# Gathered edge rows on Trainium2: a second wait in each batch of four fetches

## The chip, the cores and the metric

The kernel runs on one core of a Trainium2 chip. Its engines are PE (TensorE, matrix products, with PEld for the loading of weights), DVE (VectorE), ACT (ScalarE), POOL (GpSimd, which here issues the indirect fetches) and SP (SyncE, which issues plain transfers). Every engine works through its own list of instructions in order, and waits on semaphores for the others. The metric is the device time of one launch in microseconds (us), less being better. Times given for "runs" are medians of several launches; a profile is one launch taken by the hardware profiler.

## The reference

The reference is one layer of a graph network with 12,500 nodes of 160 channels and 400,000 edges, sorted by destination. Cut to what matters:

```python
h = relu(layernorm(x))                               # [12500, 160]
y0 = h[:, :64] @ W_l1_0 * a / 8                      # per node, a = node attribute
y1 = einsum('nuc,uv->nvc', h1, W_l1_1) * a / sqrt(32)
w  = silu(edge16 @ fc_W1 / 4) @ fc_W2 / 8            # per edge, 192 weights
mid_a = w_a * y0[src] * e0                           # four products per edge
mid_d = w_d * sum_c(y1[src] * e1) / sqrt(3)
mid_b = (w_b * y0[src])[:, :, None] * e1[:, None, :]
mid_c = (w_c * e0)[:, :, None] * y1[src]
z = segment sum of (mid_a, mid_d, mid_b, mid_c) over dst
out = x + C_S * (self part of h) + C_X * (z @ W_l2) * a
```

The part that takes the time is the middle: for each edge the row of `y` that belongs to its source node is fetched, multiplied by the edge's own weights, and added up over the edges that end in the same node.

## The kernel before

First the kernel writes the mapped node rows `y_d` to HBM (some 115 us). Then comes the main loop, which is what the change touches.

The edges are cut into 3125 tiles of 128, and four tiles (`GT = 4`) make a batch; there are 782 batches, numbered `b`. For each batch the following is done, by functions that are written out in program order in one loop over `b` and keep that order on every engine (the scheduling is manual).

- `gather(b)` on POOL: four indirect fetches (L570), one per tile; each brings the 128 rows of 160 floats that belong to a tile's sources from `y_d` into one slot of the buffer `yg`. There are six such buffers. Sixteen of the 782 batches (`xs_of`) are not fetched but worked out from `x`.
- `hidden_pair(s)` on PE (L583) and ACT (L588): the first layer of the edge network, for four batches at a time. It stands behind the sums of every fourth batch.
- `weigh(b)` on PE (L603): the second layer, two products into the PSUM tile `pw`; ACT adds five columns of edge data to it (L525).
- `products(b)` on DVE: the one-hot matrix `sel` (L617, L619) and the product rows `pr` out of `pw` and `yg` (L530, then L534 twice). This is the only reader of the fetched rows.
- `sums(b)` on PE (L633): four products `sel` times `pr`, one per tile, added up in the PSUM tile `pz`. A window of 3 to 24 tiles shares one `pz`. Behind the last tile of a window DVE turns the sums out of PSUM (L639, L640 into `za`).
- `linear`, `add` and `accumulate` once for every four windows (L646, L650, L658, L669): the last linear layer and the addition into `acc`.

In one pass for `b` the order of the code is: `weigh(b + 2)`, `linear` or `add` if due, `products(b + 1)`, `sums(b)`, `gather(b + 4)` and, for every fourth `b`, `hidden_pair`. So rows are fetched four batches ahead (`AHEAD = 4`), products are made one ahead of the sums, and weights two ahead.

What sets the pace of the fetches is one wait. The first of the four fetches of batch `b` waits on a semaphore of PE until the last product of the sums of batch `b - 4` has ended; the other three follow it on POOL's queue without a wait on PE:

```python
if k == 0 and b - AHEAD in summed:
    tc.add_manual_dep(fetch.ins, summed[b - AHEAD], ...)
```

`summed[b]` holds the name of the last product that `sums(b)` issued.

## Time and profile before

| what | value |
|---|---|
| median of three runs | 4708.81 us (4700.06 to 4720.77) |
| the profiled execution, its own time | 4710.64 us |
| its span, first to last instruction | 4708.8 us |
| fetches of the main loop on POOL (L570) | 3061, 2901.9 us busy |
| sums on PE (L633) | 1950.3 us busy |
| weights on PE (L603) | 1233.8 us busy |
| mean granted clock of TensorE | 0.906 |

How to read it: a busy time is the sum of an engine's instruction times. An "idle before" time is how long the engine stood still ahead of a group of instructions, with the event that ended the idleness behind the arrow; "issue" means that nothing in the profile released it, and "remote" or "another core or an unknown queue" that the releaser was not found among the recorded instructions near the release. The start of a matmul is recorded and its end is modelled. The granted clock of TensorE is 1 at full rate; in this trace it is either 1 or one half.

### The profile page before, as it was taken

How to read it: one execution, taken by the hardware profiler on the slowest of the kernel's cores; microseconds unless marked ns; L12 is line 12 of the kernel's file. 1: busy time of each engine (PE TensorE's matmuls, PEld its weight loads, DVE VectorE, ACT ScalarE, POOL GpSimd, SP SyncE). 2: the span in 40 equal slices, each digit the busy share in tenths (PEclk: the TensorE clock that was granted, in tenths of full speed). 3: DMA queues.
4: the chain of work that ended last, by engine and by line, in shares of the span. 5: the costliest groups of instructions: out<-in, count | busy, mean ns of one | idle time of the engine just before them, and what ended most of it. 6: DMA issues, size and time to landing. Idle time of an engine off the chain costs nothing.

```text
span 4708.8 us, 46910 instructions
## 1 busy us (share of the span) xinstructions
PE 3891.7 (83%) x14078; PEld 2542.2 (54%) x14078; DVE 2736.7 (58%) x6877; ACT 581.6 (12%) x1845; POOL 2968.3 (63%) x3145
## 2 busy tenths in 40 slices
PE   7788888888788787887888888888888888888888
PEld 6455555555555455555555555555555555555555
DVE  5555555555555555555555656556556666666665
ACT  5111111111111101101110101111011111111100
POOL 5666666666666666666666666666666666666665
PEclk8889999999999998988888989998989998998889
DMA  7222222222222222222222222222222222222224
GB/s 192 69 63 65 66 66 65 66 67 64 60 64 67 66 69 67 67 66 67 70 68 62 65 63 67 66 68 63 63 66 65 68 64 63 65 64 67 59 62 117
DMA packets 262471, 328.58 MB, mean 70 GB/s; under 512 B 82888, under 2 KB 212216, under 8 KB 262216
## 3 DMA queue, kind: packets, MB, share of 16 engines
q0 software_dynamic: 150128, 256.23, 20.5%
q1 hardware_dynamic: 111590, 69.02, 5.2%
q8 instruction: 116, 1.90, 0.2%
q14 instruction: 139, 1.14, 0.1%
q10 hardware_dynamic: 498, 0.30, 0.0%
HBM read 307.67 MB, written 17.61 MB: 69 GB/s over the span
## 4 chain that ended last, share of the span: by engine, by line
PE 66%; another core or an unknown queue 15%; issue 7%; DVE 7%; ACT 2%; ACTq 1%; POOL 0%; DMA 0%; DVEq 0%; SPq 0%; POOLq 0%
PE pz L633 31%; PE pw L603 19%; PE px L646 6%; PE px L583 3%; DVE pr L534 2%; PE px L658 2%; DVE pr L530 1%; ACT hT L588 1%; ACTq L525 1%; DVE za L640 1%; DVE za L639 1%; PE po L457 1%; PE px L704 1%; POOL yg L570 0%
## 5 line engine op out<-in xcount | busy, mean ns | idle before, releaser
L570 POOL DMA_INDIRECT yg<-y_d,src_q x3061 | 2901.9, 948 | 1681.5 <-issue 795.2
L633 PE MATMUL pz<-pr,sel 128*128 128x320 f32 x6250 | 1950.3, 457 | 17.6 <-DVE za L640 15.2
L633 PEld LDWEIGHTS pz<-pr,sel 128*128 128x128 f32 x6250 | 1243.5, 204 | 542.6 <-issue 94.9
L603 PE MATMUL pw<-w,hT 128*128 128x384 f32 x3126 | 1233.8, 519 | 208.7 <-DVE pr L534 135.6
L603 PEld LDWEIGHTS pw<-w,hT 128*128 128x128 f32 x3126 | 590.3, 198 | 734.3 <-issue 375.5
L639 DVE STREAM_TRANSPOSE za<-pz 128x160 f32<-128x160 f32 x598 | 206.5, 345 | 1298.9 <-PE pz L633 551.3
L534 DVE TENSOR_TENSOR pr<-pw,yg 128x384 f32<-128x384 f32 x1532 | 773.5, 546 | 0.0
L530 DVE TENSOR_TENSOR pr<-pw,yg 128x512 f32<-128x512 f32 x766 | 523.2, 683 | 126.8 <-DMA yg<-y_d,src_q 118.3
L646 PE MATMUL px<-wo,za 128*128 128x160 f32 x1500 | 320.2, 376 | 294.4 <-ACT hT L588 198.2
L619 DVE TENSOR_TENSOR sel<-own,pw 128x512 f32<-128x512 f32 x782 | 536.9, 687 | 28.1 <-issue 1.2
L646 PEld LDWEIGHTS px<-wo,za 128*128 128x128 f32 x1500 | 290.2, 246 | 364.7 <-ACT hT L588 226.5
L525 ACT ACTIVATE pw<-ev 128x20 f32<-128x20 f32 x782 | 149.6, 191 | 2624.1 <-PE pw L603 970.4
L588 ACT ACTIVATE hT<-px 128x512 f32<-128x512 f32 x391 | 218.5, 595 | 968.9 <-remote 648.9
L583 PE MATMUL px<-xe,w 32*128 32x512 f32 x782 | 268.9, 658 | 66.2 <-ACT os L648 38.8
L617 DVE TENSOR_TENSOR own<-iota,pw 128x128 f32<-128x128 f32 x782 | 200.0, 256 | 177.1 <-ACT pw L525 133.8
L640 DVE STREAM_TRANSPOSE za<-pz 32x160 f32<-32x160 f32 x598 | 202.1, 338 | 20.5
L658 PE MATMUL px<-os,place 128*128 128x160 f32 x600 | 122.6, 332 | 79.0 <-ACT os L648 75.8
L669 DVE SCALAR_TENSOR_TENSOR acc<-px,a_sb,acc 128x160 f32 x300 | 113.9, 380 | 113.2 <-PE px L658 70.8
L658 PEld LDWEIGHTS px<-os,place 128*128 128x128 f32 x600 | 107.0, 211 | 131.8 <-ACT os L648 91.2
L583 PEld LDWEIGHTS px<-xe,w 32*128 32x128 f32 x782 | 70.9, 187 | 176.8 <-issue 95.7
L648 ACT ACTIVATE os<-px 128x160 f32<-128x160 f32 x150 | 45.3, 302 | 359.8 <-remote 168.4
L712 DVE SCALAR_TENSOR_TENSOR acc<-px,look,acc 128x160 f32<-128x160 f32 x98 | 32.9, 377 | 95.1 <-PE pz L633 39.7
(129 smaller groups left out, 1423.7 us busy)
## 6 DMA issues: line engine op xcount, KB each, us to landing
yg<-y_d,src_q POOLq DMA_INDIRECT x3061
xe<-in_e SPq DMA_DIRECT2D x784, 32.0 KB
xs<-in_x SPq DMA_DIRECT2D x48, 160.0 KB
acc<-in_x SPq DMA_DIRECT2D x11, 640.0 KB
y_d<-ys SPq DMA_DIRECT2D x11, 640.0 KB
out<-acc SPq DMA_DIRECT2D x11, 640.0 KB
raw<-in_e SPq DMA_DIRECT2D x32, 192.0 KB
src_q<-in_src SPq DMA_DIRECT2D x32, 48.0 KB
```

The source lines that it names most:

```text
L530: nc.vector.tensor_mul(pr[:, :n, :].rearrange("p t (x u) -> p t x u", x=2)[:, :, :, 0:M0], wt[:, :n, 0:NW].rearrange("p t (x u) -> p t x u ...
L534: nc.vector.tensor_mul(pr[:, :n, D * x + M0:D * (x + 1)].rearrange("p t (c u) -> p t c u", c=3), wt[:, :n, 96 * x + M0:96 * (x + 1)].unsqu ...
L570: fetch = nc.gpsimd.indirect_dma_start(out=yg[:, slot(t), :], out_offset=None, in_=y_d, in_offset=bass.IndirectOffsetOnAxis(ap=ev4[t // BL ...
L583: nc.tensor.matmul(ph, w1[r, :], xe[r, :], start=True, stop=True)
L588: nc.scalar.activation(hT, ph, AF.Silu, scale=1.0 / math.sqrt(FC_IN))
L603: nc.tensor.matmul(pw[:, 2 * k:2 * k + m, 0:NW], hT[:, o:o + P], w2[:, :m, :], start=True, stop=True)
L619: nc.vector.tensor_tensor(sel, own[:, :n, :].unsqueeze(2).to_broadcast([P, n, 4, WN]), wt[:, :n, NW:NW + 4].unsqueeze(3).to_broadcast([P, ...
L633: mm = nc.tensor.matmul(pz[:, 0:PC], sel[:, slot(t), :, :], pr[:, slot(t), :], start=o == 0, stop=last)
L639: nc.vector.transpose(zT[g][:, :, at_w], pz[:, D:PC].rearrange("p (k u) -> p k u", k=ZK))
L640: nc.vector.transpose(zT[g][0:32, :, at_w], pz[0:32, 0:D].rearrange("p (k u) -> p k u", k=ZK))
L646: nc.tensor.matmul(po[:m, :], za[:, k, :m], wo[:, k, :], start=k == 0, stop=k == ZK - 1)
L658: nc.tensor.matmul(ps[:, h, :], place[:m, h, :], os[:m, :], start=True, stop=True)
```

## The change

Two things change, both in the issue of the fetches.

First, the fetches are issued by half batches. Behind `sums(b)` stood the four fetches of batch `b + 4`. Now stand there the third and fourth fetch of batch `b + 3`, and then the first and second fetch of batch `b + 4`.

Second, the third fetch of a batch now waits too. The first fetch of batch `m` waits, as before, for the last product of `sums(m - 4)`; the third fetch of batch `m` waits for the second of the four products of `sums(m - 3)`, which the new table `halves` names.

```diff
+        halves = {}
...
-        def gather(b):
-            yg = ygp.tile([P, GT, D], F32, name="yg")
-            rows[b] = yg
-            for k, t in enumerate(tiles_of(b)):
+        def gather(b, part=slice(0, GT)):
+            if part.start == 0:
+                rows[b] = ygp.tile([P, GT, D], F32, name="yg")
+            yg = rows[b]
+            for k, t in list(enumerate(tiles_of(b)))[part]:
                 fetch = nc.gpsimd.indirect_dma_start(
...
-                if k == 0 and b - AHEAD in summed:
-                    tc.add_manual_dep(fetch.ins, summed[b - AHEAD],
+                of = {0: summed.get(b - AHEAD), 2: halves.get(b - AHEAD + 1)}.get(k)
+                if of is not None:
+                    tc.add_manual_dep(fetch.ins, of,
...
-                summed[b] = mm.ins.name
+                (halves if k == 1 else summed)[b] = mm.ins.name
...
             sums(b)
-            if b + AHEAD < NB and b + AHEAD not in xs_of:
-                gather(b + AHEAD)
+            for m, part in ((b + AHEAD - 1, slice(2, GT)), (b + AHEAD, slice(0, 2))):
+                if AHEAD <= m < NB and m not in xs_of:
+                    gather(m, part)
```

On POOL the place shown is the middle of the first fifth of the loop. `yg_4810` and `yg_4848` are the row buffers of two batches that follow each other; a DMASW name is the completion of an earlier fetch, DVE the readers of the buffer's former content, PE the sums. Before:

```order
L570 DMA yg_4810<-y_d_60,src_q_3744 128x160 [waits DMASW4_49,DVE_49,PE_49]
L570 DMA yg_4810<-y_d_60,src_q_3744 128x160 [waits DMASW5_49]
L570 DMA yg_4810<-y_d_60,src_q_3744 128x160 [waits DMASW6_49]
L570 DMA yg_4810<-y_d_60,src_q_3744 128x160 [waits DMASW7_49]
L570 DMA yg_4848<-y_d_60,src_q_3744 128x160 [waits DMASW0_49,DVE_49,PE_49]
L570 DMA yg_4848<-y_d_60,src_q_3744 128x160 [waits DMASW1_49]
L570 DMA yg_4848<-y_d_60,src_q_3744 128x160 [waits DMASW2_49]
L570 DMA yg_4848<-y_d_60,src_q_3744 128x160 [waits DMASW3_49]
```

The order of the fetches is the same now, and the third of each batch has a wait on PE of its own. After:

```order
L572 DMA yg_4810<-y_d_60,src_q_3742 128x160 [waits DMASW4_49,DVE_49,PE_49]
L572 DMA yg_4810<-y_d_60,src_q_3742 128x160 [waits DMASW5_49]
L572 DMA yg_4810<-y_d_60,src_q_3742 128x160 [waits DMASW6_49,PE_49]
L572 DMA yg_4810<-y_d_60,src_q_3742 128x160 [waits DMASW7_49]
L572 DMA yg_4848<-y_d_60,src_q_3742 128x160 [waits DMASW0_49,DVE_49,PE_49]
L572 DMA yg_4848<-y_d_60,src_q_3742 128x160 [waits DMASW1_49]
L572 DMA yg_4848<-y_d_60,src_q_3742 128x160 [waits DMASW2_49,PE_49]
L572 DMA yg_4848<-y_d_60,src_q_3742 128x160 [waits DMASW3_49]
```

761 of the 3061 fetches of the loop get this second wait, and no fetch moved in POOL's queue.

On PE the place shown is a fourth batch, with the weights (`pw`), the four sums (`pz`) and the pair of the first layer (`px` out of `xe`) behind them. Before:

```order
L603 MATMUL pw<-w_94,hT 128x2x192 [waits DVE_49,Activation_49]
L603 MATMUL pw<-w_94,hT 128x2x192
L633 MATMUL pz<-pr,sel 128x320 [waits PE_49]
L633 MATMUL pz<-pr,sel 128x320 x3
L583 MATMUL px<-xe,w_93 128x512 [waits DMAHW3_49,DMAHW2_49]
L583 MATMUL px<-xe,w_93 128x512 [waits DMAHW5_49,DMAHW4_49,Activation_49]
L603 MATMUL pw<-w_94,hT 128x2x192 [waits DVE_49]
```

The same rows stand there now, at line numbers that are three higher. After:

```order
L606 MATMUL pw<-w_94,hT 128x2x192 [waits DVE_49,Activation_49]
L606 MATMUL pw<-w_94,hT 128x2x192
L636 MATMUL pz<-pr,sel 128x320 [waits PE_49]
L636 MATMUL pz<-pr,sel 128x320 x3
L586 MATMUL px<-xe,w_93 128x512 [waits DMAHW3_49,DMAHW2_49]
L586 MATMUL px<-xe,w_93 128x512 [waits DMAHW5_49,DMAHW4_49,Activation_49]
L606 MATMUL pw<-w_94,hT 128x2x192 [waits DVE_49]
```

Nothing moved or was added on PE, DVE, ACT and SP, and their waits are the same; the second of the four sums now has a waiter on POOL.

## The prediction

> **What bounds the kernel now.** I read the page's sums by engine first, then the chain of waits, then the waits of POOL and DVE, and last a stretch of 40 us in order of time. The first fence has the engines' busy times and the chain that ended last, by engine, from the page.
>
> ```profile
> PE 3891.7 (83%) x14078; PEld 2542.2 (54%) x14078; DVE 2736.7 (58%) x6877; ACT 581.6 (12%) x1845; POOL 2968.3 (63%) x3145
> ...
> PE 66%; another core or an unknown queue 15%; issue 7%; DVE 7%; ACT 2%; ACTq 1%; POOL 0%; DMA 0%; DVEq 0%; SPq 0%; POOLq 0%
> ```
>
> No engine is full, and 15% of the chain, some 706 us of 4708.8, has no instruction at all to show for itself. POOL looks free. The next fence shows that it is not: the fetches as one group with their first and last start, the waits of POOL (total, times, longest), and the one wait for rows on DVE.
>
> ```profile
> L570 POOL DMA_INDIRECT yg<-y_d,src_q x3061: 940/947/1236, 115.6 to 4686.4; - x192
> L570 POOLq EVENT_SEMAPHORE  x798: 17/43/205, 102.2 to 4681.2; - x200
> ...
> POOL yg L570 <- issue: 795.2, 2541, 4.6
> POOL yg L570 <- PE pz L633: 372.5, 149, 7.2
> POOL yg L570 <- remote: 314.1, 131, 3.7
> POOL yg L570 <- PE pw L603: 85.0, 66, 4.9
> ...
> DVE pr L530 <- DMA yg<-y_d,src_q: 118.3, 70, 3.0
> ```
>
> Now POOL in order of time (start, length, idle before); left out are fetches like their neighbours.
>
> ```profile
> 2524.74 0.95 POOL L570 DMA_INDIRECT yg<-y_d,src_q  x1 [4.28 <-PE pz L633]
> 2525.99 0.95 POOL L570 DMA_INDIRECT yg<-y_d,src_q  x1 [0.30 <-issue]
> ...
> 2538.53 0.94 POOL L570 DMA_INDIRECT yg<-y_d,src_q  x1 [0.30 <-issue]
> 2541.93 0.95 POOL L570 DMA_INDIRECT yg<-y_d,src_q  x1 [2.46 <-remote]
> ...
> 2545.69 0.95 POOL L570 DMA_INDIRECT yg<-y_d,src_q  x1 [0.30 <-issue]
> 2549.32 0.95 POOL L570 DMA_INDIRECT yg<-y_d,src_q  x1 [2.68 <-PE pz L633]
> ...
> 2563.10 0.94 POOL L570 DMA_INDIRECT yg<-y_d,src_q  x1 [0.30 <-issue]
> 2566.58 0.94 POOL L570 DMA_INDIRECT yg<-y_d,src_q  x1 [2.54 <-remote]
> ```
>
> A fetch holds POOL for 0.95 us and the next starts 0.30 us later: one step is 1.25 us, a batch of four 5.0 us. 3061 steps are 3826 us, and from the first fetch to the last pass 4571 us. So POOL is taken for 84% of the main loop, and its real idleness is about 745 us, which the three waits on PE hold (372.5 + 314.1 + 85.0 in 346 waits, each with 0.30 us of its step). Twelve fetches in a row, three batches, is what stands between two waits in 2524.74 to 2538.53 and in 2549.32 to 2563.10.
>
> The same time on PE:
>
> ```profile
> 2531.80 1.53 PE L603 MATMUL pw<-w,hT 128*128 128x384 f32 x4
> 2533.16 2.32 PE L633 MATMUL pz<-pr,sel 128*128 128x320 f32 x8
> 2535.41 1.13 PE L583 MATMUL px<-xe,w 32*128 32x512 f32 x4
> 2542.39 3.03 PE L646 MATMUL px<-wo,za 128*128 128x160 f32 x10 [4.37 <-ACT hT L588]
> 2545.22 3.83 PE L633 MATMUL pz<-pr,sel 128*128 128x320 f32 x8
> 2548.88 1.45 PE L603 MATMUL pw<-w,hT 128*128 128x384 f32 x4
> 2550.71 2.32 PE L633 MATMUL pz<-pr,sel 128*128 128x320 f32 x8
> 2552.87 1.45 PE L603 MATMUL pw<-w,hT 128*128 128x384 f32 x4
> 2554.16 2.32 PE L633 MATMUL pz<-pr,sel 128*128 128x320 f32 x8
> 2557.72 2.32 PE L633 MATMUL pz<-pr,sel 128*128 128x320 f32 x8
> ```
>
> And the turning out of sums on DVE, the first to use a finished sum:
>
> ```profile
> 2528.50 0.35 DVE L639 STREAM_TRANSPOSE za<-pz 128x160 f32<-128x160 f32 x1
> 2541.70 0.35 DVE L639 STREAM_TRANSPOSE za<-pz 128x160 f32<-128x160 f32 x1 [2.64 <-remote]
> 2566.34 0.35 DVE L639 STREAM_TRANSPOSE za<-pz 128x160 f32<-128x160 f32 x1 [6.07 <-remote]
> ```
>
> And on ACT the use of the weights of 2531.80:
>
> ```profile
> 2533.41 0.19 ACT L525 ACTIVATE pw<-ev 128x20 f32<-128x20 f32 x1 [3.38 <-PE pw L603]
> ```
>
> At full clock PE makes a batch in 3.45 us (2550.71 to 2554.16), against POOL's 5.0. So POOL falls behind and runs without a pause, until PE itself stands. How it comes to stand is the odd thing. At 2528.50, four microseconds into the row, DVE finds its sum ready (no idle time stands ahead of it), and at 2533.41 ACT takes the weights as soon as they are done. But the sums that start at 2533.16 have all left PE by 2535.48, but DVE takes them up at 2541.70, and POOL starts at 2541.93. The sums of 2557.72 to 2560.04 are taken up at 2566.34. Both times the release comes 2.2 to 2.3 us behind the end of POOL's last fetch (2538.53 + 0.94 and 2563.10 + 0.94), with POOL ten or more microseconds into an unbroken row of fetches. I read it so: the signals of PE are held up once POOL has fetched long enough without a break, and come through only when POOL has run dry. Why, the trace doesn't show. The Trainium skill ("Perfetto Trace Analysis", Per-instruction lifecycle) says that a matmul's reported end is an estimate and that its signal goes out when PSUM has acknowledged the write; a late signal could then also be a late matmul, which no row here tells apart.
>
> Behind such a stop PE's clock is low, as the table of windows shows (span, busy time of PE, PEld, DVE, ACT, POOL, granted clock, DMA):
>
> ```profile
> 2541.70:2549.30 7.60, 6.91 (x20) 5.49 (x21) 3.55 (x9) 1.47 (x4) 3.79 (x4) 0.57 0.37 104
> 2549.30:2556.50 7.20, 7.20 (x29) 4.80 (x28) 6.61 (x16) 1.24 (x6) 5.66 (x6) 1.00 0.21 58
> 2556.50:2566.30 9.80, 6.08 (x20) 3.00 (x20) 3.70 (x9) 0.19 (x1) 5.71 (x7) 0.95 0.22 59
> ```
>
> One round is thus 24.6 us for four batches (16 fetches): 20 us of fetching and two waits of POOL, one for a held signal and one for a sum on the slow clock. POOL and PE take turns in binding the kernel.
>
> **The change part by part.** *The reordering* moves no instruction on any queue: 0 us. *The wait as an instruction*: waits beyond the first show as separate instructions of 43 ns on POOL's sequencer; 761 more are at most 33 us. In the stretch the fetches keep their 0.30 us whether or not such a wait lies between them, since it is worked off while the fetch before it runs. I take 0 and keep 0 to 33. PE's side, a signal more from the second of four sums, has no row of its own; the nearest is that the sums start every 3.45 us with the signal they have, so 0, and 0 as the other end.
>
> *The wait itself, where PE is ahead of POOL*, binds nothing: the half sums are long done. That is most of an unbroken row. *Where POOL is ahead*, it now stops before the third fetch too. Take 2541.93: two fetches end at 2544.4, the half of the sums of 2545.22 ends at some 2547.0, and the other two fetches then run to 2549.6, where the next batch's first could before start at 2549.32. The idle time is not doubled but moved from before the first to before the third fetch; what is lost is two fetches, 2.5 us, less the second half of the sums: on the slow clock (2545.22 to 2548.88, half 1.8) 0.7 us, at full clock (2550.71 to 2552.87, half 1.1) 1.4 us. There are 346 such restarts. Queued behind the waiting fetch stand the rest of the row; who waits for these are DVE's products, and through them PE.
>
> What of it reaches the end? (1) *Through rows that come late*: DVE waits for rows in 70 of 766 batches, 9%. 346 x 0.7 to 1.4 is 242 to 484 us of POOL, of which 9% are 22 to 44; I take 33. That cover, rows fetched four batches ahead, is what hides the rest. (2) *Through a later release*: 131 waits of POOL end by a releaser not found, the held signals, and these end a fixed time behind POOL's last fetch. A row of fetches that runs 0.7 to 1.4 us later releases PE that much later: 92 to 183 us. I take 92, since the first restart after a release is on the slow clock (0.57). (3) *A gain*: if the signal of the half sums is held with the rest, POOL runs dry two fetches sooner, and the release comes 2.5 us sooner: up to 131 x 2.5 = 328 us; never held it gives 0. In the stretch the signal of the weights got through at 2533.41 and that of the sums at 2535.48 did not; the half, at 2534.4, may lie on either side, so one in two. The two fetches are still to be made after the release, which costs nothing only where POOL waits again soon (149 waits for a sum beside 131 held: again one in two). A quarter of 328 is 82.
>
> The sum: 33 + 92 - 82 = +43 us on the span of 4708.8. The profiled launch took 4710.64 us, 0.04% over the median of 4708.81, so no correction: **4752 us**, or 0.9% slower. With its own bounds (rows 22 to 44, release 92 to 183, gain 0 to 82) the likeliest case lies between 4741 and 4936.
>
> **The rivals.** *It is hidden anyway* (no change): rows come four batches ahead and 91% of the batches don't wait for them; if neither the row's end nor the held signals move, only 22 us remain: 4731, at most 0.5%. Against it speaks that POOL is taken for 84% of the time. That the change doesn't do what it says can only be so as far as POOL is behind anyway; that gives the same number.
>
> *Shorter holds* (faster): the half's signal is held nearly every time and the two fetches fit into the wait that follows (2.68 us at 2549.32). Then 0.8 of 328 us are won, 262, less 33 and the smaller 92: 4708.8 - 262 + 125 = 4572. It decides from the point where more than 0.38 of the 131 holds (125 of 328 us) begin before the half and have a wait behind them to fill. For it speaks that a release 2.5 us sooner also shortens PE's standing still. The Trainium skill ("TensorE: Matmul & The Clock Gate", Part 1, the HAM clock gate) says that PE's clock halves after an idle window of about 3.4 us. The trace agrees that the clock is low behind each stop (0.57). By that rule a hold of 6.2 us (2535.48 to 2541.70) that shrinks to 3.7 would still mostly lose the clock, and one of 4 to 5 us would keep it, which would add to this rival.
>
> *More stops per fetch* (much slower): the rows of fetches get shorter because work comes in halves, while each stop keeps its 2.5 us. With 12 in place of 16 fetches to the two waits of a round (2.46 + 2.68 us less their steps, 4.5 us), a fetch costs 4.5/12 - 4.5/16 = 0.094 us more: 3061 x 0.094 = 288 us, 4997. For it speaks that POOL would be ahead at two places per batch; against it that PE outruns POOL at full clock, which keeps rows unbroken.
>
> **How the numbers follow.** Chances: the likeliest case 0.37, more stops 0.20, hidden 0.15, shorter holds 0.28. A measurement of this kernel tells about 0.5% (24 us) from no change. So faster 0.28, same 0.15, slower 0.57. The range for 8 in 10 takes in most of the shorter holds and most of the other end: 4580 to 4960.
>
> **What would show it.** In the profile after: the rows of fetches and their waits, of which some 350 more should stand ahead of a third fetch, with POOL's idle time on PE above 771 us; the wait of DVE for rows above 118 us; the unexplained part of the chain (15%) a little larger. Shorter holds would show as a smaller unexplained part and a clock above 0.906. Wrong I would be if holding doesn't hang on POOL's row of fetches at all, or if a second wait per batch breaks the rows before the holding sets in.

## The result and the profile after

The changed kernel takes 4684.55 us (median of 20 runs, 4667.56 to 4704.85) against 4704.53 us for the kernel before (20 runs, 4682.42 to 4721.85). The ratio is 0.996, with a 95% interval of 0.9946 to 0.9974: faster by 0.4%, where the prediction had slower by 0.9%. The profiled launch has a span of 4675.4 us at a mean granted clock of 0.918; before it was 4708.8 us at 0.906.

First the engines' busy times and the chain that ended last, from the page of the kernel after.

```profile
PE 3864.8 (83%) x14078; PEld 2499.7 (53%) x14078; DVE 2741.7 (59%) x6877; ACT 585.3 (13%) x1845; POOL 2971.7 (64%) x3145
...
PE 63%; DVE 11%; another core or an unknown queue 11%; issue 10%; ACT 2%; ACTq 1%; DVEq 1%; POOL 0%; DMA 0%; SPq 0%; POOLq 0%
```

The part of the chain without an instruction fell from 15% to 11%, by the rounded shares from some 706 to some 514 us (in a second profile of the changed kernel it is 12%). Most of that did not come off the time: PE's part fell too, from 66% to 63%, but DVE's rose from 7% to 11% and "issue" from 7% to 10%, and the span is only 33 us shorter.

Now the groups by line (busy time and mean length, then the idle time before them and what ended it). Of the kernel before, the fetches:

```profile
L570 POOL DMA_INDIRECT yg<-y_d,src_q x3061 | 2901.9, 948 | 1681.5 <-issue 795.2 <-PE pz L633 372.5 <-remote 314.1
```

And of the kernel after, the fetches and the first product on DVE that reads the rows:

```profile
L572 POOL DMA_INDIRECT yg<-y_d,src_q x3061 | 2905.4, 949 | 1644.8 <-issue 768.4 <-PE pz L636 349.1 <-remote 239.3
...
L530 DVE TENSOR_TENSOR pr<-pw,yg 128x512 f32<-128x512 f32 x766 | 524.5, 685 | 226.2 <-DMA yg<-y_d,src_q 215.9 <-issue 9.5
```

POOL makes the same 3061 fetches at the same length. Busy and idle time of this one group add up to 4583.4 us before and 4550.2 after, 33.2 us less, and the span is 33.4 us shorter. So the account of the change can be read on POOL: whatever makes its stops shorter or fewer is the gain. This is bookkeeping, not yet a cause. The waits in detail, after (total, times, longest):

```profile
POOL yg L572 <- PE pz L636: 349.1, 210, 8.0
POOL yg L572 <- remote: 239.3, 103, 3.4
POOL yg L572 <- PE pw L606: 136.3, 116, 3.3
...
DVE pr L530 <- DMA yg<-y_d,src_q: 215.9, 135, 3.0
```

The same three kinds of wait that made 771.6 us in 346 waits make 724.7 us in 429: more waits, but shorter ones, and fewer of the held kind (131 to 103). Against that DVE now waits for rows in 135 batches, not 70, and for 215.9 us, not 118.3.

POOL in order of time, two rounds of the kernel after (left out are fetches like their neighbours):

```profile
2545.71 0.95 POOL L572 DMA_INDIRECT yg<-y_d,src_q  x1 [0.30 <-issue]
2549.28 0.94 POOL L572 DMA_INDIRECT yg<-y_d,src_q  x1 [2.62 <-remote]
...
2554.29 0.95 POOL L572 DMA_INDIRECT yg<-y_d,src_q  x1 [0.30 <-PE pz L636]
...
2563.06 0.94 POOL L572 DMA_INDIRECT yg<-y_d,src_q  x1 [0.30 <-issue]
2566.48 0.95 POOL L572 DMA_INDIRECT yg<-y_d,src_q  x1 [2.47 <-remote]
...
2570.24 0.94 POOL L572 DMA_INDIRECT yg<-y_d,src_q  x1 [0.30 <-issue]
2572.08 0.95 POOL L572 DMA_INDIRECT yg<-y_d,src_q  x1 [0.90 <-issue]
```

The picture of before is still there: a row of twelve fetches (2549.28 to 2563.06) and a stop of 2.5 us that ends with a held signal. DVE takes up the finished sums at that moment and not before:

```profile
2549.11 0.35 DVE L642 STREAM_TRANSPOSE za<-pz 128x160 f32<-128x160 f32 x1 [3.67 <-remote]
2566.30 0.35 DVE L642 STREAM_TRANSPOSE za<-pz 128x160 f32<-128x160 f32 x1 [5.25 <-remote]
```

The trace's records of semaphore updates, from which the waits are worked out, say what a held signal is. In the kernel before, PE's four pieces of work that ended from 2535.48 to 2538.02 have their four updates between 2541.68 and 2541.82: DVE takes up the work at once, at 2541.70, and it is PE's update that comes late, four in a burst. Over the whole main loop of before, 719 of 2126 recorded updates by PE come more than 1 us after the last end of PE that could have made them, but only 1 of 2213 by DVE and none of 973 by ACT. After the change it is 719 of 2712. Whether PE's result or only its signal is late, these records don't say.

What is new is where the stops stand. The fetches come in fours, so the place of each in its batch can be counted off over all 3061 rows (a stop is a gap of more than 0.45 us). Before, all 347 stops, 841 us, stand before a first fetch. After, 300 of them, 717 us, stand before a third fetch and 56, 92 us, before a first one. The stops of the fence are all before third fetches, the one at 2572.08 being a short one, 0.90 us in place of 0.30; the third fetch at 2554.29 doesn't stop. So the main stop moved by half a batch, became shorter in sum, and some fifty small stops came on top.

### The profile page after: what moved, and what is told of

It is laid out like the page before. It is cut to its first block, busy times and chain, and to the rows that moved or that the text cites. A ratio compares the mean times of both kernels' runs of the same rounds, so it can differ in the third digit from the quotient of the medians.

```text
span 4675.4 us, 47671 instructions
## 1 busy us (share of the span) xinstructions
PE 3864.8 (83%) x14078; PEld 2499.7 (53%) x14078; DVE 2741.7 (59%) x6877; ACT 585.3 (13%) x1845; POOL 2971.7 (64%) x3145
## 4 chain that ended last, share of the span: by engine, by line
PE 63%; DVE 11%; another core or an unknown queue 11%; issue 10%; ACT 2%; ACTq 1%; DVEq 1%; POOL 0%; DMA 0%; SPq 0%; POOLq 0%
PE pz L636 29%; PE pw L606 20%; PE px L649 5%; DVE pr L534 4%; PE px L586 3%; DVE pr L530 2%; PE px L661 2%; DVE za L643 1%; DVE za L642 1%; ACT hT L591 1%; ACTq L525 1%; DVE own L620 1%; DVE sel L622 1%; PE px L707 1%
## 5 line engine op out<-in xcount | busy, mean ns | idle before, releaser
L636 PE MATMUL pz<-pr,sel 128*128 128x320 f32 x6250 | 1926.4, 453 | 19.6 <-DVE za L643 13.9
L606 PE MATMUL pw<-w,hT 128*128 128x384 f32 x3126 | 1255.5, 527 | 350.9 <-DVE pr L534 169.7
L636 PEld LDWEIGHTS pz<-pr,sel 128*128 128x128 f32 x6250 | 1227.2, 202 | 542.1 <-issue 91.4
L530 DVE TENSOR_TENSOR pr<-pw,yg 128x512 f32<-128x512 f32 x766 | 524.5, 685 | 226.2 <-DMA yg<-y_d,src_q 215.9
L649 PE MATMUL px<-wo,za 128*128 128x160 f32 x1500 | 295.9, 356 | 199.1 <-ACT hT L591 114.7
L649 PEld LDWEIGHTS px<-wo,za 128*128 128x128 f32 x1500 | 273.8, 233 | 263.7 <-ACT hT L591 136.7
```

Source lines behind the costliest of these rows:

```text
L530: nc.vector.tensor_mul(pr[:, :n, :].rearrange("p t (x u) -> p t x u", x=2)[:, :, :, 0:M0], wt[:, :n, 0:NW].rearrange("p t (x u) -> p t x u ...
L606: nc.tensor.matmul(pw[:, 2 * k:2 * k + m, 0:NW], hT[:, o:o + P], w2[:, :m, :], start=True, stop=True)
L636: mm = nc.tensor.matmul(pz[:, 0:PC], sel[:, slot(t), :, :], pr[:, slot(t), :], start=o == 0, stop=last)
L649: nc.tensor.matmul(po[:m, :], za[:, k, :m], wo[:, k, :], start=k == 0, stop=k == ZK - 1)
```

## The experiments

Theory 1: while POOL runs a long unbroken row of indirect fetches, signals of the other engines are held until the row ends; waits at half batches let POOL stop and start in smaller steps and so gain, and the later rows take a part back. Its rivals: A, the holds are PE's own and POOL's rows don't matter; B, only the distance counts by which POOL may run ahead; C, the additional wait instruction itself changed something; D, the moment of the wait within a batch. All ratios are to runs of the kernel before on the same chip, with a 95% interval.

**No pace at all.** The wait of the first fetch is taken out; only the six row buffers hold POOL back.

```diff
-                if k == 0 and b - AHEAD in summed:
+                if False:
```

> The kernel before without any wait of a fetch on the sums: only the six buffers of rows hold POOL back. Theory 1 (signals are held while POOL runs an unbroken row of fetches, so a finer pace that breaks the rows gains): rows grow beyond the 4 to 16 fetches of before, more signals are held and longer, and the kernel takes 1.01 to 1.03 of before, 4750 to 4850 us. Rival A (the holds are PE's own, around sums followed by a hidden pair, and POOL's rows don't matter): the pace is only a cost, 0.98 to 1.00 of before. Rival B (what counts is how far POOL may run ahead, since fetches that come early only take room from PE's and DVE's other work): slower too, in step with the distance, about 1.01.

Measured: 5177.46 us, ratio 1.1 (1.0974 to 1.1026). The chain, then POOL's largest wait that is not "issue", and ACT's wait for weights without a releaser:

```profile
PE 52%; another core or an unknown queue 22%; DVE 11%; issue 9%; POOL 2%; ACT 2%; ACTq 1%; DVEq 0%; DMA 0%; SPq 0%; POOLq 0%
```

```profile
POOL yg L570 <- DVE pr L534: 761.9, 161, 13.6
...
ACT pw L525 <- remote: 838.9, 119, 29.9
```

Letting POOL run costs 10%, more than theory 1 had for it: the unexplained part is some 1139 us (22%), and ACT stood idle up to 29.9 us ahead of its use of the weights with no releaser to be found. Rival A, for which a pace is only a cost, falls, and the loss is ten times what rival B had (1.01). The wait on the sums keeps the kernel before from losing 475 us.

**The second wait where it cannot bind.** The third fetch waits for the half of the batch for which the first fetch has waited already.

```diff
-                of = {0: summed.get(b - AHEAD), 2: halves.get(b - AHEAD + 1)}.get(k)
+                of = {0: summed.get(b - AHEAD), 2: halves.get(b - AHEAD)}.get(k)
```

> The changed kernel, but the third fetch of a batch waits for the first half of the sums of the batch four in front, which the first fetch of the same batch has already waited for: the extra waits and their order stay and none can bind. Theory 1: rows are those of before, 0.998 to 1.002 of before, and about 1.004 of the changed kernel. Rival C (the second wait instruction itself or its place is what moved the time): 0.996 of before, as the changed kernel.

Measured: 4701.37 us, ratio 1.0006 (0.9989 to 1.0023). The instruction and the new order cost and gain nothing; rival C falls.

**The new wait alone**, in whole steps of four fetches from the middle of one batch to the middle of the next.

```diff
-                of = {0: summed.get(b - AHEAD), 2: halves.get(b - AHEAD + 1)}.get(k)
+                of = {2: halves.get(b - AHEAD + 1)}.get(k)
```

> The changed kernel with the new wait alone: the first fetch of a batch waits for no sum. POOL gets leave for four fetches at a time as before, only shifted by half a batch, so its rows have 4, 8, 12 or 16 fetches. Theory 1 (finer steps gain): 0.998 to 1.003 of before. Rival D (the moment of the wait within the batch is what gains, not the finer step): 0.994 to 0.998 of before. Rival B (the distance): the distance in fetches and sums is the same as before, so 0.998 to 1.002.

Measured: 4721.04 us, ratio 1.0037 (1.0016 to 1.0058): a small loss, so rival D falls, and theory 1's own band is missed at the upper end. A likely reason is DVE's wait for rows, which is that of the changed kernel:

```profile
DVE pr L530 <- DMA yg<-y_d,src_q: 212.3, 128, 3.7
```

**One fetch at a time.** Each fetch waits for one sum more: the first for the last sum of the batch four in front, the others for the first, second and third sum of the batch three in front.

```diff
-                of = {0: summed.get(b - AHEAD), 2: halves.get(b - AHEAD + 1)}.get(k)
+                of = summed.get(b - AHEAD) if k == 0 else parts.get((b - AHEAD + 1, k - 1))
...
-                (halves if k == 1 else summed)[b] = mm.ins.name
+                (parts if k < 3 else summed)[(b, k) if k < 3 else b] = mm.ins.name
...
-            for m, part in ((b + AHEAD - 1, slice(2, GT)), (b + AHEAD, slice(0, 2))):
+            for m, part in ((b + AHEAD - 1, slice(1, GT)), (b + AHEAD, slice(0, 1))):
```

> Finer still: each fetch waits for one sum more, the first of a batch for the last sum of the batch four in front, the second, third and fourth for the first, second and third sum of the batch three in front. Theory 1: rows break at single fetches, the long rows in which all signals are held become fewer, and the time falls once more, 0.988 to 0.994 of before (4650 to 4680 us). The prediction's own term for later rows (0.7 to 1.4 us at each restart of POOL) would make it slower than the changed kernel, 0.998 to 1.01 of before, if nothing is won by shorter rows.

Measured: 4690.29 us, ratio 0.9974 (0.9953 to 0.9995). It is not below the changed kernel, so theory 1's 0.988 to 0.994 is missed. The prediction's price for restarts gave 0.998 to 1.01, which the measured interval touches at its lower end only. DVE waits still longer for rows:

```profile
DVE pr L530 <- DMA yg<-y_d,src_q: 282.1, 184, 3.3
```

Here theory 1 had to be cut in two. The change does two things at once: the step becomes finer, and the last fetch of a batch is let go later. The next two kernels move them apart; the changed kernel was run beside them once more.

**Half steps with the full distance.** The first fetch waits for the first half of the batch four in front, the third for the rest of it. So the last two fetches are let go as in the kernel before.

```diff
-                of = {0: summed.get(b - AHEAD), 2: halves.get(b - AHEAD + 1)}.get(k)
+                of = {0: halves.get(b - AHEAD), 2: summed.get(b - AHEAD)}.get(k)
...
-            for m, part in ((b + AHEAD - 1, slice(2, GT)), (b + AHEAD, slice(0, 2))):
+            for m, part in ((b + AHEAD, slice(0, 2)), (b + AHEAD, slice(2, GT))):
```

> Half batches with the longer distance once more (first fetch for the first half of the sums of the batch four in front, third for the rest). Where nothing is held: 1.000 of before, as measured. Where signals are held: theory 1 (the finer step gains by itself) 0.992 to 0.998 and VectorE's wait for rows near 118 us; rival B (the distance gains) 1.003 to 1.02 and an unexplained part of the chain of 15% or more.

Measured: 4675.52 us, ratio 0.9937 (0.9913 to 0.9961), as theory 1 had it and not as rival B had it. DVE's wait for rows is less than half of that before, and the unexplained part is 11%, as in the changed kernel:

```profile
PE 67%; another core or an unknown queue 11%; DVE 9%; issue 9%; ACT 2%; DMA 1%; ACTq 1%; DVEq 0%; POOL 0%; SPq 0%; POOLq 0%
```

```profile
DVE pr L530 <- DMA yg<-y_d,src_q: 49.7, 34, 2.5
```

**The changed kernel again**, without an edit.

> The changed kernel once more, beside the kernel before on the chip that this run gets. Two chips have run the kernel before at 4702 and at 3956 us; on the second no signal is held and POOL ran 2992 fetches without a stop. Theory 1 (the change trades shorter holds for later rows): where signals are held, 0.994 to 0.998 of before once more; where none is held only the later rows are left, 1.003 to 1.02 of before, VectorE's wait for rows above the 953 us of the half-batch kernel with the full distance. Rival C (the change gains whatever is held): below 1 on both.

Measured: 4686.74 us, ratio 0.9964 (0.9949 to 0.998), the first result once more.

**Three batches ahead**, whole steps.

```diff
-AHEAD = 4
+AHEAD = 3
```

> Whole batches with POOL three batches in front once more. Where nothing is held: 1.029 of before, as measured. Where signals are held: rival B (the distance) an unexplained part below 11%, VectorE's wait for rows above 300 us, 0.99 to 1.02 of before; theory 1 (the finer step) an unexplained part above 12%, 1.01 to 1.03.

Measured: 4718.72 us, ratio 1.0033 (1.0019 to 1.0046). The unexplained part is the smallest of the paced kernels so far, and DVE's wait for rows the largest:

```profile
PE 34%; issue 20%; DVE 16%; POOL 15%; another core or an unknown queue 7%; DMA 5%; ACT 1%; DVEq 1%; ACTq 1%; POOLq 0%; SPq 0%
```

```profile
DVE pr L530 <- DMA yg<-y_d,src_q: 906.8, 468, 5.7
```

All three are what rival B had, and theory 1's own marks (above 12%, 1.01 to 1.03) are missed. So rival B has a point, in that the distance trades one for the other, but alone it gains nothing.

Put together, the runs read as a table of two things: the step, and how many tiles may lie between the last fetch of a batch and the newest sum that is sure to have ended when it starts (worked out from the waits: before, the fourth fetch of batch m, tile 4m+3, needs the sum of tile 4m-13, so 16).

| kernel | step, fetches | lead of a batch's last fetch, tiles | DVE's wait for rows, us | POOL's main stops | its other stops | ratio |
|---|---|---|---|---|---|---|
| before | 4 | 16 | 118.3 | 347, 841 us | 0 | 1 |
| half steps, full distance | 2 | 16 | 49.7 | 315, 756 us | 38, 52 us | 0.9937 |
| new wait alone | 4 | 14 | 212.3 | 306, 842 us | 11, 10 us | 1.0037 |
| the change | 2 | 14 | 215.9 | 300, 717 us | 56, 92 us | 0.996 |
| one at a time | 1 | 13 | 282.1 | 313, 725 us | 127, 125 us | 0.9974 |
| three batches ahead | 4 | 12 | 906.8 | 331, 859 us | 0 | 1.0033 |

The stops are counted as above; the main ones stand before one and the same fetch of the batch in each kernel. The finer step adds some forty to sixty small stops (1.4 to 1.6 us each) and takes 85 us (lead 16) and 125 us (lead 14) off the main ones, more than it adds; that short pauses in a row shorten what follows is tried by itself further below. In the second profile of the change, with a span of 4691.9 us, the main stops are 741 us and the others 93, so such sums differ by some 25 us from launch to launch. The wait for rows grows with every tile of lead that is lost. At equal lead the half step takes off 0.63% (lead 16) and 0.77% (lead 14: 0.996 to 1.0037); at equal step the lost lead adds 0.37% (step 4) and 0.23% (step 2; 0.27% side by side on one chip). The two effects are of opposite sign and within their intervals of the same size in both rows and both columns, so the change is their sum. The intervals of the two kernels with half steps overlap, so the price of the lead at step 2 is likely rather than certain. A step of one fetch adds more small stops and takes nothing more off the main ones.

**Do holds hang on the rows of fetches?** The second and fourth fetch of each batch become plain loads from SyncE's queue (half the gather is left out).

```diff
+PLAIN = (1, 3)
...
+                if k in PLAIN:
+                    nc.sync.dma_start(yg[:, slot(t), :], y_d[t * P % (N - P):t * P % (N - P) + P, :])
+                    continue
```

> The kernel before, with the second and fourth fetch of each batch replaced by a plain load of 128 rows of the same table from SyncE's queue (it leaves out the gather of half the rows; bytes and everything else stay). Theory 1 (signals are held while POOL runs an unbroken row of fetches): POOL's work halves to about 1913 us, its rows become short, the part of the chain of waits that shows no instruction falls from 15% to under 5%, and the time falls to 4000 to 4250 us, near PE's 3892 us busy. Rival A (PE's own holds): that part stays at 12% or more and the time at 4550 us or more.

> The second and fourth fetch of a batch as plain loads from SyncE's queue once more (half the gather is left out). Where nothing is held: 0.893 of before, as measured, 3532 us. Where signals are held: theory 1 (holds hang on POOL's unbroken rows, which are two fetches long here) 3530 to 3700 us, the unexplained part under 3%; rival A (PE's own holds, or the chip's, whatever POOL does) 4000 us or more with 10% or more unexplained.

The two runs came to different chips, and that gave the surprise of this study. On the one, the kernel before itself took 4701.87 us, as everywhere so far; there the kernel with two fetches took 3551.08 us, ratio 0.7547 (0.7523 to 0.7571). On the other the kernel before took 3955.59 us, and this one 3531.78, ratio 0.8928 (0.8915 to 0.8942). The chain on the chip where the kernel before takes 4702 us:

```profile
PE 88%; DVE 7%; issue 2%; ACT 0%; DVEq 0%; DMA 0%; ACTq 0%
```

Nothing is unexplained, and the two chips agree within 0.6%. So with rows of two fetches no signal is held: none of 2191 updates by PE in the loop is more than 1 us late. Rival A falls here too. This kernel halves the number of fetches as well as the rows' length, and doesn't tell these two apart; the pause every 4 fetches, further below, does.

**The chip on which nothing is held.** Three more kernels ran there beside the kernel before at 3955.59 us (3953.86 to 3960.01): half steps with the full distance, three batches ahead, and the kernel before with a break in the row, for which every eighth fetch waits for the landing of the one ahead of it.

```diff
+                if k == 0 and b % 2 and landed:
+                    tc.add_manual_dep(fetch.ins, landed[-1], ...)
+                landed.append(fetch.ins.name)
```

> Half batches as in the changed kernel, but with the distance on the other side: the first fetch of a batch waits for the first half of the sums of the batch four in front, the third for the rest of them. The third and fourth are let go as in before, the first and second half a batch earlier. Theory 1 (the finer step gains by itself): 0.992 to 0.998 of before, the wait of VectorE for rows stays at about 118 us. Rival B (the distance gains, the fine step nothing): POOL is let go earlier, rows grow, holds are longer, 1.003 to 1.015, and the unexplained part of the chain is 15% or more.

> The kernel before with POOL three batches ahead of the sums in place of four, whole batches as before. Rival B (the distance): the unexplained part falls below the 11% of the changed kernel, VectorE waits for rows above 300 us, and the sum of the two is 0.99 to 1.02 of before. Theory 1 (the finer step): rows of four fetches stay, the unexplained part stays above 12%, later rows are added, 1.01 to 1.03.

> The kernel before, with one wait more: every eighth fetch waits until the rows of the fetch ahead of it have landed (2.3 us after its start), so that no row of fetches is longer than 8, each broken by a stop of 1 to 2 us. It adds 382 stops, some 400 to 700 us, to the 3826 us of POOL's steps. Theory 1: holds seldom begin before 8 us of an unbroken row, so the unexplained part of the chain falls from 15% to 8% or less, while rows come no later than before as long as POOL keeps up: 0.98 to 0.995 of before. Rivals A and B (holds don't hang on the row's length; or only the distance counts): POOL is the fuller for nothing, 1.01 to 1.06.

Measured: 0.9996 (0.9987 to 1.0005), 1.029 (1.0273 to 1.0307) and 1.2151 (1.2135 to 1.2168). The first and the last lie outside every band that was expected, all of which supposed that signals are held. The second lies in theory 1's band, but without the unexplained 12% that went with it. Of the first, the fetches as a group, the chain, and POOL in order of time:

```profile
L572 POOL DMA_INDIRECT yg<-y_d,src_q x3061 | 2901.9, 948 | 941.7 <-issue 588.9 <-PE pw L606 119.7 <-PE pz L636 69.4
```

```profile
PE 31%; DMA 25%; DVE 21%; issue 14%; POOL 8%; DVEq 1%; ACT 0%; SPq 0%; POOLq 0%; ACTq 0%
```

```profile
2500.18 0.95 POOL L572 DMA_INDIRECT yg<-y_d,src_q  x1 [0.30 <-issue]
2501.43 0.94 POOL L572 DMA_INDIRECT yg<-y_d,src_q  x1 [0.30 <-PE pz L636]
...
2538.96 0.95 POOL L572 DMA_INDIRECT yg<-y_d,src_q  x1 [0.31 <-issue]
```

POOL steps through the whole loop at 1.25 us (idle time of 941.7 us for 3061 fetches is 0.31 us each); one row is 2992 fetches long, and yet no wait in this trace has an unknown releaser, and none of 3362 updates by PE in the loop is more than 1 us late. POOL's steps alone are the bound: 99 us before the first fetch and 3826 us of steps are nearly all of the span of 3952. A stop that is added there is paid in full. POOL's idle time is 120 us longer with three batches ahead and 858 us longer with the break, and the times are 119 and 851 us longer than that of the half steps. So the half step has nothing to gain. And an unbroken row is not enough for a hold; something of the chip belongs to it, which no row shows. Each chip was measured at one time only, so that the chip and the hour are not told apart. Fetches are as long on both (948 ns).

**What ends a hold?** On the other chips a hold mostly ended when POOL stood still (nine in ten of the updates over 2 us late in the kernel before). Three kernels, all from the kernel before, put pauses into the row: every eighth fetch waits for the landing of the fetch two ahead of it; every fourth does; or POOL writes zeros to a spare tile `rest` of 128 x 1000 ahead of every eighth fetch. The first and the last of the three edits (the second has `k == 0` alone):

```diff
+                if k == 0 and b % 2 and len(landed) > 1:
+                    tc.add_manual_dep(fetch.ins, landed[-2], ...)
+                landed.append(fetch.ins.name)
```

```diff
+                if k == 0 and b % 2:
+                    nc.gpsimd.memset(rest, 0.0)
```

> The kernel before, with one wait more: the first fetch of every second batch waits until the rows of the fetch two ahead of it have landed. After the 2.4 us stop of the kernel that waited for the fetch just ahead, this one should stop POOL about 1.2 us, every 8 fetches: 382 stops, some 0.9 us beyond the usual 0.3 each, +340 us of POOL's work on 3826. Theory 1 with its second half (a pause of 1 us lets all held signals go, and POOL then never runs out of leave): where signals are held, 4250 to 4400 us, 0.90 to 0.94 of before, nearly nothing unexplained in the chain. Rival E (only a stop in which every fetch has landed, 2.4 us, lets signals go): 1.00 to 1.08 of before, since holds and pauses add. Where nothing is held: 3956 + 340, about 1.085 of before.

> The same pause ahead of every batch, every 4 fetches: 765 stops, +690 us of POOL's work. Theory 1: 4600 to 4700 us, POOL is the bound and nothing is unexplained, 0.98 to 1.00 of before, slower than with a pause every 8. Rival E: above 1.05 of before. Where nothing is held: about 1.17.

> The kernel before, with a memset of 128x1000 on POOL ahead of every eighth fetch in place of a wait: POOL is busy with something that is no fetch for about 1 us (382 times, some 400 to 500 us of its work). If it is a pause between fetches that lets signals go, whatever POOL does in it: as with the pause every 8, 4250 to 4450 us where signals are held. If POOL must be idle or its queue of fetches drained: 1.00 to 1.10 of before. Where nothing is held: about 1.10.

Measured: the pause every 8 fetches 4633.69 us, 0.9822 (0.9789 to 0.9854); every 4, 4781.32 us, 1.014 (1.0107 to 1.0174); the memset every 8, 4623.75 us, 0.9795 (0.9759 to 0.9831). The groups of POOL with the memset, and its chain:

```profile
L574 POOL DMA_INDIRECT yg<-y_d,src_q x3061 | 2908.2, 950 | 1236.9 <-issue 775.8 <-remote 154.0 <-PE pz L637 132.3
L573 POOL MEMSET rest<- 128x1000 f32 x375 | 356.5, 951 | 0.1
```

```profile
PE 62%; another core or an unknown queue 11%; DVE 10%; issue 10%; POOL 2%; ACT 1%; DVEq 1%; DMA 1%; ACTq 0%; POOLq 0%
```

POOL is given 356.5 us of idle work, and the sum of its fetches, memsets and idle time falls from 4583.4 to 4501.6 us. It is not the idleness of POOL that counts but the pause between fetches, with the same gain whether it waits or works. But the theory wanted 0.90 to 0.94, and the rival for which only a stop of 2.4 us lets signals go wanted 1.00 or more: pauses of 1.1 to 1.2 us every 8 fetches shorten holds and don't end them. 11% stay unexplained, and 721 updates by PE are over 1 us late in either kernel, as many as before; only those over 2 us fell, from 505 to 328 and 348.

With the pause every 4 fetches the holds are gone, on the same chip and with all 3061 fetches: none of 1808 updates by PE in the loop is more than 1 us late, and no wait of the loop has an unknown releaser. So the length of the unbroken row decides there, not the number of fetches. The price is paid elsewhere. POOL's steps and pauses alone come to some 4591 us, by an estimate from these rows (115 and 3061 times 1.25, and 765 times the 0.85 by which a pause of 1.15 exceeds the usual 0.30), and DVE waits for rows in 701 batches. Theory 1's 4600 to 4700 us is missed by 81 us:

```profile
DVE pr L530 <- DMA yg<-y_d,src_q: 1859.7, 701, 6.5
```

**Shorter pauses, and both remedies together.** A memset of a `rest` of 128 x 500 ahead of every fourth fetch; and the memset of 128 x 1000 every eighth fetch in the kernel with half steps and full distance.

```diff
+                if k == 0:
+                    nc.gpsimd.memset(rest, 0.0)
```

> The kernel before with a memset of half the size, 128x500, about 0.48 us, ahead of every fourth fetch: the same sum of pauses as with 128x1000 every eighth, spread more evenly. If it is the share of POOL's time without fetches that counts (a backlog that drains): 0.975 to 0.985 of before, as there. If a pause has to last about 1 us to let anything go: 1.00 to 1.06, since 0.5 us only adds. Where nothing is held: 1.08 to 1.10.

> The half batches with the full distance (0.994 of before where signals are held) and the memset of 128x1000 ahead of every eighth fetch (0.980) together. If the two gains are separate: 0.970 to 0.976 of before, 4560 to 4590 us. If the pauses already break the rows that the half step breaks: 0.978 to 0.985. Where nothing is held: 1.09 to 1.10.

Measured: 4669.88 us, 0.9865 (0.9841 to 0.989), and 4722.22 us, 0.9975 (0.996 to 0.9989). The evenly spread pauses (410.0 us in 766 memsets of 535 ns, most with 0.70 us between two fetches) gain less than 356.5 us in pieces of 0.95 us did on another chip, but they gain, so a pause need not last a microsecond; the ratio lies between the two bands that were expected. The two remedies together gained less than either did alone, and less than either expectation had (0.970 to 0.985). The three ratios come from three chips, so a part of this may be the chip's. That the memset takes the place at which the half step gains is a guess; no run shows it.

The kernel with the memset every 8 fetches is thus the fastest of those that compute everything, 2% under the kernel before and 1.7% under the changed one (0.9795 to 0.996), where signals are held; the same pause by a wait (0.9822) lies within its interval. Where none are held, it was not run; its 356.5 us of memsets would there stand in POOL's bound, by an estimate from that row some 9% of 3956 us.

## Why the prediction was wrong

It named the parts rightly and took all three terms too large, the later release most, so that the sign of the sum came out wrong. The measured 4684.55 us lies in the range of 4580 to 4960, but only because that range reaches far to both sides of no change. Step by step:

- *What bounds the kernel*: POOL's 1.25 us per fetch and held signals in turn. Borne out: with half the fetches the time falls to 3551 us with nothing unexplained, and without a pace it rises to 5177. What the traces of these chips could not show is that an unbroken row alone holds nothing: one chip ran 2992 fetches without a hold.
- *The reordering*, 0, and *the wait as an instruction*, 0 of 0 to 33 us: right, 1.0006 (0.9989 to 1.0023).
- *Term (1), rows that come late*, +33 (22 to 44): right in kind and sign, too large. DVE's wait for rows rose by 97.6 us (118.3 to 215.9), but the price of the lost lead, which holds everything that a later second half costs, is 0.23 to 0.37%, 11 to 17 us.
- *Term (2), a later release*, +92: this is the step that failed. It had the stops move to the third fetch, which 300 of 356 did, and each restart behind a hold lose 0.7 us or more by that. But the main stops are no longer than before (717 us in 300, 2.39 each, to 841 in 347, 2.42 each), and held waits of POOL fell from 314.1 us in 131 to 239.3 us in 103. The price of the lost lead, 11 to 17 us, covers this term together with (1) when the runs are split in this way, so that at most some 17 of the 92 us came. With (2) at nothing the sum, 33 - 82, has the right sign; with (3) at its measured size and (2) left as it was, it has not. A part of the reason is that where the third fetch asks, as at 2554.29, the half sums can have ended already; how often, was not counted.
- *Term (3), the gain of a shorter hold*, -82 (0 to -328): the right sign, but too large: the half step at equal lead is worth 0.63 to 0.77%, -30 to -36 us with its small stops, under half of what I took.
- The sum by the measured sizes, 11 to 17 less 30 to 36, is -13 to -25 us, and the medians differ by 20. That is no separate test, since 0.996, the result itself, is one of the four ratios behind these sizes.
- *Shorter holds*, the rival with the right sign: its 4572 us was far too low, since a tenth of the 328 us came, not 0.8 of it. Its point of decision, 0.38 of the holds, was wrong too, because it set the gain against 125 us of losses, terms (1) and (2), that were only 11 to 17.
- *More stops per fetch* (4997): there are more waits on PE, 429 for 346, but each shorter, and the finest step, one fetch, still is no slower than before (0.9974). *Hidden anyway* (4731) had a small change, and the change is small, but for another reason: two effects of some 15 and 33 us cancel in part.
- *What would show it*: POOL's idle time on PE was to go above 771 us and went to 724.7; the unexplained part was to grow and fell to 11%; DVE's wait for rows above 118 us held. Both marks of shorter holds that I had named, the smaller unexplained part and the clock above 0.906, are there. Third fetches did get their stops, 300 of them, but in place of those before first fetches and not beside them. The last sentence of the prediction, that a second wait may break the rows before the holding sets in, comes nearest to what the small stops do.
- One reading is loose: the three waits hold 668 of POOL's 745 idle us (771.6 less 0.30 in each of 346), not all of them. No term uses the difference.

The clock is higher than before (0.918 for 0.906) and higher still with fewer holds (0.93 with three batches ahead, 0.995 with half the fetches). The Trainium skill ("TensorE: Matmul & The Clock Gate", Part 1, the HAM clock gate) has the clock halve after an idle window; these runs agree in direction, and the time did not follow the clock: three batches ahead has the higher clock and is slower.

## What to carry to other kernels

When a change adds a wait, ask two separate questions: in how fine a step does it let the waiting engine go, and how late is the last piece of a unit of work let go; here these had opposite signs, and the version that kept the lead and took only the finer step (0.9937) came out ahead of the change (0.9964) beside it, though their intervals overlap. A price per restart, multiplied by the number of restarts, was far above what was paid here: look first whether the event waited for has already happened when the wait is reached. And where a part of the chain has no instruction, test it by thinning out the queue that runs meanwhile, before building a sum on it.

## What the runs showed of the hardware

- On four of five chips the semaphore updates of PE come late while POOL runs indirect fetches in an unbroken row (719 of 2126 by more than 1 us in the kernel before), and those of DVE and ACT don't (1 of 2213, none of 973). Counted over all windows and weights of the kernel before, where the reader stood idle and the end of PE's work lay inside a row of fetches: of those that ended 4 to 6 us into the row 7% were taken up more than 1 us late, at 8 to 10 us 68%, from 12 us on all.
- This depends on the chip. On the five chips of the experiments the kernel before ran at 4702.47, 4701.87, 4712.55, 4732.23 and 3955.59 us; only on the last was nothing held, in a row of 2992 fetches. A profile from one chip can hide what bounds the kernel on another. What the difference is stays open, and each chip was measured at one time only.
- A pause between fetches relieves it in part, whether POOL waits or writes a tile: 1.1 us every 8 fetches took 1.8 to 2.1% off, 0.7 us every 4 fetches 1.35%. A pause of some 1.15 us every 4 fetches left no update of PE more than 1 us late, but cost 1.4% in all.
- The Trainium skill ("SBUF — State Buffer", Who interferes with whom) says that only the port pair that VectorE and GpSimd share causes contention, and that a fetch issued by GpSimd can starve there. The fetches shown here keep 948 to 950 ns on both kinds of chip, so that is not what is seen; what comes late is PE's update of its semaphore. Why it does, no run found.
